# Weight loads on ScalarE's queue and weight preparation in steps, in a two-layer row attention kernel

## The chip, the cores and the metric

The kernel runs on one core of a Trainium2 chip. The metric is the time of one execution on the device in microseconds, as a median over runs; four runs of the kernel before gave 3379.72 us (3377.62 to 3380.11). The profile is one further execution, recorded by the hardware profiler.

The engines are named as in the profile: PE is TensorE (PEld its weight loads), DVE is VectorE, ACT is ScalarE, POOL is GpSimd, SP is SyncE, which only issues transfers. "SPq" and "ACTq" are the queues through which SP and ScalarE issue transfers (DMA). A line number L1144 is line 1144 of the kernel before.

## The reference

The input x has 128 rows of 256 positions with 256 channels, z has 256 x 256 positions with 128 channels. Layer 0 is attention within each row, with a bias worked out from z; layer 1 is banded attention. Cut to what matters here:

```python
def _gn(v, G=32, eps=1e-5):            # mean and variance of a group of 8 channels over all rows and positions
    g = v.reshape(B_, H_, W_, G, C_ // G)
    m = jnp.mean(g, axis=(1, 2, 4), keepdims=True)
    s = jnp.var(g, axis=(1, 2, 4), keepdims=True)
    return ((g - m) / jnp.sqrt(s + eps)).reshape(v.shape)

# layer 0, on m = _gn(x)
m_norm = layer_norm(m, ln_m_w, ln_m_b)
z_norm = layer_norm(z, ln_z_w, ln_z_b)
q, k, v = m_norm @ Wq.T, m_norm @ Wk.T, m_norm @ Wv.T        # 8 heads of 32
b = (z_norm @ Wb.T).transpose(0, 3, 1, 2)[:, None]
gate = sigmoid(m @ Wg.T + bg)
scores = einsum('bsihc,bsjhc->bshij', q, k) * scale + b
o = einsum('bshij,bsjhc->bsihc', softmax(scores), v) * gate
x = x + o @ Wo.T + bo

# layer 1, on _gn of the new x: 4 heads of 64, band of 16
qkv = x2 @ w_in.T + b_in
x = x + banded_attention(qkv) @ w_out.T + b_out
```

The group norm needs a sum over the whole of x before the first row can be projected, and the bias needs all of z. So the kernel begins with a pass over all of x and z.

## The kernel before, in words

The kernel is `fast_kernel`, with a general kernel behind it that runs only if a test of value ranges at the end asks for it. It has three parts: the opening (to about 246 us), layer 0 over 64 pairs of rows (to about 2115 us), layer 1 over 64 pairs.

**The weights** (lines 828 to 939). `load_chunks`, `load_col` and `load_row` load a matrix, a vector as columns (elements of 4 bytes) and a vector copied to all partitions. All of them issue through SP's queue, and so do w_out (8 loads), wb, and bv_c (4 loads). They are 27 loads with 2.3 MB in all; wq, wk, wv, wg, wo and w_out have 256 KB each, w_in 768 KB.

**Their preparation** (lines 996 to 1055). The layer norms' weights and biases are folded into the matrices. The products of the biases with wq, wk, wv and wb (`qb`, `kb`, `vb_r`, `bz_r`: lines 998 to 1017) are matrix products on PE, copied out by DVE. Then wq, wk, wv are scaled by `lnw_c` (1020 to 1022), and the mean of their columns, by a product with the constant matrix `avg` on PE (1028), is subtracted on DVE (1030); wb is treated in the same way (1031, 1039, 1040), and four copies of it are laid into `wbz` (1055). Smaller scalings of w_in, bin_c, bg_c and wo come along (1023, 1032 to 1035). The products use the pool `ps_mm`, which has two buffers in PSUM: a third product waits until DVE has read the first.

**The pass over z and x** (lines 1470 to 1492). The order of each engine's instructions between `with tc.manual_schedule()` and its end is the order in which the code is written; instructions outside of it are placed by the scheduler, also among or ahead of those inside. z comes in 16 jobs of 2 MB, x in 8 blocks of 4 MB:

- `z_front` loads a z tile (`zt`, three buffers, line 1061) and takes its statistics on DVE in 16 instructions (1069), then their scale `zrs` (1077 on DVE, 1078 on POOL). After each quarter of the statistics it calls `mark`, at which steps of other work are taken in by a table, `plan`.
- `z_back` of the job before turns the tile on PE (32 transposes, 1091), copies it with ScalarE (1093), and projects it with `wbz` (1106). When the transposes are done, the tile's buffer is free for the job three further on.
- `x_block` loads a block (`xa`, two buffers, 1142) and takes its statistics in 16 instructions on DVE (1144).

Job 0 is followed by x block 0, jobs 2 to 8 each by one of the blocks 1 to 7; job 1 has none. So the order on DVE is z0, x0, z1, z2, x1, z3, x2, z4, x3 and so on to z8, x7, z9 to z15. SP's queue issues the loads in the same order, and each waits there until its buffer is free: z3 until PE has turned z0, x2 until DVE is through with x0. What stands behind a waiting load in the queue waits too.

After x7, `x_moments` (1151 to 1156) merges the sums of x; the table `plan` then spreads the group norm's constants and the first pair's preparation over jobs 9 to 15. When z is done, layer 0 begins.

Line 1616, `bv_w`, belongs to the preparation of layer 1. It multiplies `ones` by `bv_c` on DVE, outside of the hand-written order.

Of the kernel before, what the change touches and what calls it, by code (L numbers as in the profile page):

```python
# [9 lines left out]
F32 = mybir.dt.float32  # L10
AF = mybir.ActivationFunctionType
ALU = mybir.AluOpType
# [4 lines left out]
P = 128  # L17
# [756 lines left out]
def fast_kernel(  # L774
# [46 lines left out]
    ones = const.tile([P, P], F32, name="ones")  # L821
    nc.vector.memset(ones, 1.0)
    avg = const.tile([P, P], F32, name="avg")
# [3 lines left out]

    def load_chunks(src, n, name):
        t = const.tile([P, src.shape[0] // P, n], F32, name=name)
        nc.sync.dma_start(t, src.rearrange("(k p) n -> p k n", p=P))  # L830
        return t

    def load_col(src, name):
        t = const.tile([P, src.shape[0] // P], F32, name=name)
        nc.sync.dma_start(t, src.rearrange("(k p) -> p k", p=P))
        return t

    def load_row(src, name):
        n = src.shape[0]
        t = const.tile([P, n], F32, name=name)  # L840
        nc.sync.dma_start(t, src.unsqueeze(0).broadcast_to([P, n]))
        return t


# [63 lines left out]

    eb = const.tile([P, H, NB, I], F32, name="eb")

    wq = load_chunks(wqT, C, "wq")
    wk = load_chunks(wkT, C, "wk")
    wv = load_chunks(wvT, C, "wv")
    wg = load_chunks(wgT, C, "wg")
    wo = load_chunks(woT, C, "wo")
    w_in = load_chunks(w_inT, 3 * C, "w_in")

    w_out = const.tile([P, KC, C], F32, name="w_out")
    for a in range(KC):
        for h in range(H1):  # L920
            n = P // H1
            nc.sync.dma_start(w_out[h * n : (h + 1) * n, a, :], w_outT[(2 * h + a) * n : (2 * h + a + 1) * n, :])
    wb = const.tile([CZ, H], F32, name="wb")
    nc.sync.dma_start(wb, wbT)
    lnw_c = load_col(ln_m_w, "lnw_c")
    lnb_c = load_col(ln_m_b, "lnb_c")
    lzw_c = load_col(ln_z_w, "lzw_c")
    lzb_c = load_col(ln_z_b, "lzb_c")
    bg_c = load_col(bg, "bg_c")
    bin_c = load_col(b_in[0 : 2 * C], "bin_c")  # L930
    bo_r = load_row(bo, "bo_r")
    bv_c = const.tile([P, KC], F32, name="bv_c")
    for h in range(H1):
        n = P // H1
        nc.sync.dma_start(
            bv_c[h * n : (h + 1) * n, :],
            b_in[2 * C + h * D1 : 2 * C + (h + 1) * D1].rearrange("(a i) -> i a", i=n),
        )
    bout_r = load_row(b_out, "bout_r")

    qb = const.tile([P, KC], F32, name="qb")
    kb = const.tile([P, KC], F32, name="kb")
    vb_r = const.tile([P, C], F32, name="vb_r")
    bz_r = const.tile([P, H], F32, name="bz_r")
# [12 lines left out]
    def group_pairs(src, g):  # L957

        return src[:, :, g * GE : (g + 2) * GE].rearrange("p n (h e) -> p n e h", h=2)
# [27 lines left out]
    pz = tc.alloc_tile_pool(name="pre_z", bufs=1, side="right")  # L987
# [4 lines left out]
    def mm(name):  # L992
        return ps_mm.tile([P, 512], F32, name=name, tag="mm")


    lnb_w = pz.tile([P, KC, P], F32, name="lnb_w")
    for k in range(KC):
        nc.vector.tensor_scalar_mul(lnb_w[:, k, :], ones, lnb_c[:, k : k + 1])
    for w, dst in ((wq, qb), (wk, kb)):
        for m in range(KC):  # L1000
            ps = mm("b_ps")
            for k in range(KC):
                nc.tensor.matmul(
                    ps[:, 0:1], w[:, k, m * P : (m + 1) * P], lnb_c[:, k : k + 1],
                    start=(k == 0), stop=(k == KC - 1),
                )
            nc.vector.tensor_copy(dst[:, m : m + 1], ps[:, 0:1])
    nc.vector.tensor_scalar_mul(qb, qb, QS)
    ps = mm("b_ps")
    for k in range(KC):  # L1010
        nc.tensor.matmul(ps[:, :C], lnb_w[:, k, :], wv[:, k, :], start=(k == 0), stop=(k == KC - 1))
    nc.vector.tensor_copy(vb_r, ps[:, :C])
    lzb_w = pz.tile([P, P], F32, name="lzb_w")
    nc.vector.tensor_scalar_mul(lzb_w, ones, lzb_c)
    ps = mm("b_ps")
    nc.tensor.matmul(ps[:, :H], lzb_w, wb, start=True, stop=True)
    nc.vector.tensor_copy(bz_r, ps[:, :H])

    for k in range(KC):
        nc.vector.tensor_scalar(wq[:, k, :], wq[:, k, :], lnw_c[:, k : k + 1], QS, ALU.mult, ALU.mult)  # L1020
        nc.vector.tensor_scalar_mul(wk[:, k, :], wk[:, k, :], lnw_c[:, k : k + 1])
        nc.vector.tensor_scalar_mul(wv[:, k, :], wv[:, k, :], lnw_c[:, k : k + 1])
        nc.vector.tensor_scalar_mul(w_in[:, k, 0:C], w_in[:, k, 0:C], QS1)

    for w in (wq, wk, wv):
        ps = mm("b_ps")
        for k in range(KC):
            nc.tensor.matmul(ps[:, :C], avg, w[:, k, :], start=(k == 0), stop=(k == KC - 1))
        for k in range(KC):
            nc.vector.scalar_tensor_tensor(w[:, k, :], ps[:, :C], -1.0 / KC, w[:, k, :], ALU.mult, ALU.add)  # L1030
    nc.vector.tensor_scalar_mul(wb, wb, lzw_c)
    nc.vector.tensor_scalar_mul(bin_c[:, 0:KC], bin_c[:, 0:KC], QS1)

    nc.vector.tensor_scalar_mul(bg_c, bg_c, 0.5)
    nc.vector.tensor_scalar_mul(wo.rearrange("p k n -> p (k n)"), wo.rearrange("p k n -> p (k n)"), 0.5)


    ps = mm("b_ps")
    nc.tensor.matmul(ps[:, :H], avg, wb, start=True, stop=True)
    nc.vector.tensor_sub(wb, wb, ps[:, :H])  # L1040

    nga = S // GA
    st0 = pz.tile([P, nga, G, 3], F32, name="st0")
# [5 lines left out]
    IB, IS = 32, 64  # L1049
    zjobs = [(b, i) for b in range(NB) for i in range(0, I, IB)]  # L1050
    z_rows = z.rearrange("(u t) (p b) c -> t p u (b c)", t=NB, b=NB)
    wbz = pz.tile([P, 4, 4, H], F32, name="wbz")
    nc.vector.memset(wbz, 0.0)
    for j in range(4):
        nc.vector.tensor_copy(wbz[:, j, j, :], wb)

    def z_front(b, i0):

        nonlocal zrs
        zt = pz.tile([P, IB, CZ], F32, name="zt", tag="zt", bufs=3)  # L1060
        nc.sync.dma_start(
            zt.rearrange("p (u b) c -> p u (b c)", b=NB), z_rows[b, :, i0 // NB : (i0 + IB) // NB, :]
        )

        st = pz.tile([P, IB, 3], F32, name="zst", tag="zst", bufs=2)
        for i in range(0, IB, 2):
            if i % (IB // 4) == 0 and i:
                mark(i // (IB // 4))
            nc.vector.bn_stats(
                st[:, i : i + 2, :].rearrange("p i f -> p (i f)"),  # L1070
                zt[:, i : i + 2, :].rearrange("p i c -> p c i"),
            )
        at = i0 % IS
        if at == 0:
            zrs = pz.tile([P, IS], F32, name="zrs", tag="zrs", bufs=3)
        rs = zrs[:, at : at + IB]
        nc.vector.tensor_scalar(rs, st[:, :, 2], 1.0 / CZ, 1e-5, ALU.mult, ALU.add)
        nc.gpsimd.tensor_tensor(rs, rs, mhalf[:, :IB], ALU.pow)
        return zt, zrs
# [60 lines left out]
    def x_block(j):  # L1140
        xa = px.tile([P, GA * NB, C], F32, name="xa", tag="xa", bufs=2)
        nc.sync.dma_start(xa, x[j * GA : (j + 1) * GA].rearrange("s i c -> (s i) c").rearrange("(p n) c -> p n c", p=P))
        for g in range(0, G, 2):
            nc.vector.bn_stats(st0[:, j, g : g + 2, :].rearrange("p g f -> p (g f)"), group_pairs(xa, g))  # L1144

    def x_moments():
# [316 lines left out]
    ended = None  # L1463

    def mark(quarter):
        if ended is not None:
            plan.pop((n - ended, quarter), nothing)()


    behind, nx, n = None, 0, 0  # L1470
    with tc.manual_schedule():
        for n, job in enumerate(zjobs):
            front = z_front(*job)
            if behind is not None:
                z_back(*behind)
            behind = (*job, *front)
            if nx < nga and nx * 9 <= n * nga:
                x_block(nx)
                nx += 1
                if nx == nga:  # L1480
                    ended = n
            mark(4)
        assert not plan
        z_back(*behind)
        z_project()
        z_exp()
# [14 lines left out]
    with tc.manual_schedule():  # L1501
        old = was = Nobody()
        es = nn3 = None
        for p in range(NP):
# [3 lines left out]
            ps = now.scores(0, 0)  # L1508
# [15 lines left out]
            ps = now.scores(0, 1)  # L1524
# [13 lines left out]
            ps = now.scores(1, 0)  # L1538
# [12 lines left out]
            ps = now.scores(1, 1)  # L1551
# [52 lines left out]
    with tc.tile_pool(name="l1", bufs=2) as sb, tc.tile_pool(  # L1604
        name="l1s", bufs=4
# [310 lines left out]
```

## Time and profile before

| | us |
|---|---|
| median of four runs | 3379.72 |
| profiled execution | 3377.75 |
| its span, first to last instruction | 3375.9 |
| first z load issued / landed for DVE | 17.58 / 28.25 |
| preparation of the weights on DVE | 14.44 to 27.24 |
| statistics of x block 0 / block 7 begin | 38.03 / 155.20 |
| first scores of layer 0 used by DVE (line 1305) | 247.00 |

Busy time over the whole span: PE 3229.2 us (96%), DVE 2027.1 (60%), POOL 1973.0 (58%), ACT 1463.1 (43%); the DMA engines moved 262.89 MB. The 40 equal slices of the span (84 us each) show that the beginning differs from the rest: in tenths of busy time PE has 5, 3, 8, 9 and then 9 throughout, DVE 7, 9, 6, 6, and the DMA engines 9, 9, 5, 1 and then 1 or 2.

In a row of the timeline stand the start, the time from the first start to the last end, the engine, the line, the operation, what it writes and reads, how many instructions are merged into the row, and in brackets how long the engine was idle before it and what ended that. The tables of windows give the busy time of each engine in a stretch, the number of instructions in brackets, then the granted TensorE clock, the busy share of the DMA engines and the rate in GB/s. A DMA queue's line has its packets, MB, and the time of its packets as a share of 16 engines.

### The profile page before, as it was taken

What the parts mean: (1) busy time and instruction counts of PE and PEld (TensorE: products, weight loads), DVE (VectorE), ACT (ScalarE), POOL (GpSimd) and SP (SyncE); (2) the same over time, 40 slices, a digit from 0 to 9 for tenths busy, and PEclk for the clock granted to TensorE, in tenths of its full rate; (3) what the DMA queues carried; (4) which work ended last, traced back from release to release, by engine and by line L of the source; (5) the groups of instructions that cost most, each with busy time, mean ns of one, the idle gap of its engine ahead of it and who ended that gap; (6) DMA issues with size and microseconds to landing.
All of it is one profiled execution on the core that took longest, in us unless ns stands there. A gap on an engine that the chain in (4) does not pass through costs nothing. (4 is left out here: it accounts for less than half of the span.)

```text
span 3375.9 us, 81186 instructions
## 1 busy us (share of the span) xinstructions
PE 3229.2 (96%) x35158; PEld 2036.5 (60%) x35158; DVE 2027.1 (60%) x3218; ACT 1463.1 (43%) x2121; POOL 1973.0 (58%) x1377
## 2 busy tenths in 40 slices
PE   5389999999999999999999998899999999999998
PEld 3255555555555555555555554576767767777676
DVE  7966666666666666666666666366544344444456
ACT  2264444444444444444444443344444444444443
POOL 2378877777777877877777784333333333333332
PEclk8799999999999999999999999899999999999999
DMA  9951212221221222222222211121121211211211
GB/s 333 382 135 42 73 48 74 73 73 49 73 70 47 67 70 73 48 73 73 73 48 73 73 55 57 56 65 53 54 63 52 64 54 52 65 52 58 59 58 53
DMA packets 198815, 262.89 MB, mean 78 GB/s; under 512 B 46289, under 2 KB 147537, under 8 KB 197297
## 3 DMA queue, kind: packets, MB, share of 16 engines
q1 hardware_dynamic: 197776, 257.35, 25.1%
q8 instruction: 278, 4.55, 0.7%
q14 instruction: 89, 0.72, 0.1%
q10 hardware_dynamic: 672, 0.26, 0.0%
HBM read 188.82 MB, written 68.75 MB: 76 GB/s over the span
## 5 line engine op out<-in xcount | busy, mean ns | idle before, releaser
L1310 POOL TENSOR_TENSOR eboth<-e 128x512 f32<-128x512 f32 x512 | 639.8, 1271 | 377.7 <-DVE e L1305 365.8
L1305 DVE TENSOR_TENSOR e<-ps_sc,eb 128x1024 f32<-128x1024 f32 x512 | 603.2, 1220 | 316.0 <-ACT ps_sc L1296 226.8
L1296 ACT ACTIVATE ps_sc<-ps_sc 128x1024 f32<-128x1024 f32 x512 | 492.8, 1006 | 507.5 <-PE ps_sc L1289 507.5
L1705 POOL TENSOR_TENSOR e<-e,bw 128x384 f32<-128x384 f32 x256 | 259.0, 1033 | 443.3 <-ACT e L1703 443.3
L1666 PE MATMUL ps_p<-xgT,w_in 128*128 128x512 f32 x1024 | 469.4, 601 | 0.0
L1658 POOL TENSOR_TENSOR xt<-xt,bout_r 128x1024 f32<-128x1024 f32 x64 | 152.3, 2379 | 383.9 <-PE ps_x L1655 383.9
L1758 DVE TENSOR_TENSOR yo<-ps_y,xt 128x512 f32<-128x512 f32 x128 | 88.4, 690 | 379.2 <-PE ps_y L1754 370.8
L1666 PEld LDWEIGHTS ps_p<-xgT,w_in 128*128 128x128 f32 x1024 | 188.9, 190 | 199.9 <-issue 166.6
L1289 PE MATMUL ps_sc<-qT,kT 32*128 32x256 f32 x4096 | 293.8, 400 | 2.0 <-ACT kT L1259 2.0
L1320 PE MATMUL ps_ov<-e,v 128*32 128x256 f32 x4096 | 274.1, 385 | 0.5 <-DVE oT L1334 0.5
L1255 PE MATMUL ps_p<-xnT,wq 128*128 128x512 f32 x512 | 254.3, 618 | 0.8 <-POOL xnT L1242 0.6
L1255 PE MATMUL ps_p<-xgT,wg 128*128 128x512 f32 x512 | 253.9, 618 | 0.0
L1754 PE MATMUL ps_y<-w_out,oT 128*128 128x256 f32 x1024 | 248.6, 386 | 2.6 <-DVE oT L1739 2.6
L1362 PE MATMUL ps_y<-wo,oT 128*128 128x256 f32 x1024 | 243.6, 381 | 7.0 <-POOL oT L1352 7.0
L1362 PEld LDWEIGHTS ps_y<-wo,oT 128*128 128x128 f32 x1024 | 195.4, 191 | 87.9 <-issue 59.5
L1289 PEld LDWEIGHTS ps_sc<-qT,kT 32*128 32x128 f32 x4096 | 185.4, 184 | 94.4 <-issue 70.8
L1270 PE MATMUL ps_v<-wv,xnT 128*128 128x256 f32 x1024 | 242.1, 379 | 0.0
L1255 PE MATMUL ps_p<-xnT,wk 128*128 128x512 f32 x512 | 240.6, 592 | 0.0
L1681 PE MATMUL ps_v<-w_in,xgT 128*128 128x256 f32 x1024 | 231.8, 379 | 0.0
L1736 DVE RECIPROCAL rv<-odd 128x256 f32<-128x256 f32 x128 | 224.4, 1753 | 4.4
L1681 PEld LDWEIGHTS ps_v<-w_in,xgT 128*128 128x128 f32 x1024 | 194.4, 190 | 53.5 <-issue 30.1
L1270 PEld LDWEIGHTS ps_v<-wv,xnT 128*128 128x128 f32 x1024 | 189.6, 190 | 50.9 <-issue 31.1
(163 smaller groups left out, 4992.0 us busy)
## 6 DMA issues: line engine op xcount, KB each, us to landing
zt<-in_z_dram SPq DMA_DIRECT2D x16, 2048.0 KB
xa<-in_x_dram SPq DMA_DIRECT2D x8, 4096.0 KB
xt<-in_x_dram SPq DMA_DIRECT2D x64, 512.0 KB
rvb<-rsum SPq DMA_DIRECT2D x256, 128.0 KB
x<-xo SPq DMA_DIRECT2D x16, 2048.0 KB
xt<-x SPq DMA_DIRECT2D x64, 512.0 KB
out_dram<-yo SPq DMA_DIRECT2D x63, 512.0 KB
rs_r<-rs_d SPq DMA_DIRECT2D x63, 256.0 KB
```

The lines of the kernel that those rows point to most:

```text
L1255: nc.tensor.matmul(ps, w[:, k, m * P : (m + 1) * P], getattr(self, src)[:, k, :], start=(k == 0), stop=(k == KC - 1),)
L1270: nc.tensor.matmul(self.ps_v[:, b * C : (b + 1) * C], self.xnT[:, k, t * P : (t + 1) * P], wv[:, k, :], start=(k == 0), stop=(k == KC - 1),)
L1289: nc.tensor.matmul(self.pss[q // 2][:, q % 2, b, :], self.kT[rs, c, r * I + b * P : r * I + (b + 1) * P], self.qT[rs, c, r * I : (r + 1) * I],
L1296: nc.scalar.activation(self.pss[a], self.pss[a], AF.Exp)
L1305: nc.vector.tensor_tensor(e, pss[a], eb[:, h : h + 2], ALU.mult)
L1310: nc.gpsimd.tensor_tensor(t, es[a][:, :, 0, :], es[a][:, :, 1, :], ALU.add)
L1320: nc.tensor.matmul(ov[q * D0 : (q + 1) * D0, :], self.v[:, r, b, h * D0 : (h + 1) * D0], es[q // 2][:, q % 2, b, :], start=(b == 0), stop= ...
L1362: nc.tensor.matmul(self.ps_y[:, b * C : (b + 1) * C], self.oT[r][:, k, b * P : (b + 1) * P], wo[:, k, :], start=(k == 0), stop=(k == KC - 1),)
L1666: nc.tensor.matmul(ps, w_in[:, k, n * C + m * P : n * C + (m + 1) * P], self.xgT[:, k, :], start=(k == 0), stop=(k == KC - 1),)
L1681: nc.tensor.matmul(ps[:, b * C : (b + 1) * C], self.xgT[:, k, t * P : (t + 1) * P], w_in[:, k, 2 * C : 3 * C], start=(k == 0), stop=(k == ...
L1705: nc.gpsimd.tensor_tensor(e[:, q], e[:, q], bcast(bw.rearrange("p b w -> p (b w)"), 1, KC), ALU.mult)
L1754: nc.tensor.matmul(ps[:, b * C : (b + 1) * C], self.oT[r][:, k, b * P : (b + 1) * P], w_out[:, k, :], start=(k == 0), stop=(k == KC - 1),)
```

## The change

Three things are changed.

1. All weight loads are issued through ScalarE's queue (`nc.scalar.dma_start`) instead of SP's, and their order is new: lnb_c, wq, wk, wv, wb, lnw_c, lzw_c, lzb_c, wg, wo, w_in, w_out, bg_c, bin_c, bo_r, bv_c, bout_r. So SP's first loads are z tile 0 and x block 0.
2. Tile 0 of z is loaded as two halves, each with a transfer of its own.
3. The preparation becomes a generator, `weights()`, whose steps are taken inside of the hand-written order: three among the statistics of x block 0 (after each quarter but the last), three at the quarters of z job 1, and one at the end of job 1. Between two steps PE makes the products that the next one reads. `z_back` of job 0, the first user of `wbz`, comes after step 6.

```diff
     def load_chunks(src, n, name):
-        nc.sync.dma_start(t, src.rearrange("(k p) n -> p k n", p=P))
+        nc.scalar.dma_start(t, src.rearrange("(k p) n -> p k n", p=P))
...
+    def weights():
+        lnb_w = pz.tile([P, KC, P], F32, name="lnb_w")
         for k in range(KC):
+            nc.vector.tensor_scalar_mul(lnb_w[:, k, :], ones, lnb_c[:, k : k + 1])
+        for w, dst in ((wq, qb), (wk, kb)):
+            pss = []
+            for m in range(KC):
+                ps = mm("b_ps")
+                for k in range(KC):
+                    nc.tensor.matmul(
+                        ps[:, 0:1], w[:, k, m * P : (m + 1) * P], lnb_c[:, k : k + 1],
+                        start=(k == 0), stop=(k == KC - 1),
+                    )
+                pss.append(ps)
+            yield
+            for m in range(KC):
+                nc.vector.tensor_copy(dst[:, m : m + 1], pss[m][:, 0:1])
+        nc.vector.tensor_scalar_mul(qb, qb, QS)
+        ps_v = mm("b_ps")
...
+        ps_z = mm("b_ps")
+        nc.tensor.matmul(ps_z[:, :H], lzb_w, wb, start=True, stop=True)
+        yield
+        nc.vector.tensor_copy(vb_r, ps_v[:, :C])
+        nc.vector.tensor_copy(bz_r, ps_z[:, :H])
+        for k in range(KC):
+            nc.vector.tensor_scalar(wq[:, k, :], wq[:, k, :], lnw_c[:, k : k + 1], QS, ALU.mult, ALU.mult)
+            nc.vector.tensor_scalar_mul(wk[:, k, :], wk[:, k, :], lnw_c[:, k : k + 1])
+            nc.vector.tensor_scalar_mul(wv[:, k, :], wv[:, k, :], lnw_c[:, k : k + 1])
+        nc.vector.tensor_scalar_mul(wb, wb, lzw_c)
+        for ws in ((wq, wk), (wv,)):
+            pss = []
+            for w in ws:
+                ps = mm("b_ps")
+                for k in range(KC):
+                    nc.tensor.matmul(ps[:, :C], avg, w[:, k, :], start=(k == 0), stop=(k == KC - 1))
+                pss.append(ps)
+            if ws == (wv,):
+                ps_b = mm("b_ps")
+                nc.tensor.matmul(ps_b[:, :H], avg, wb, start=True, stop=True)
+            yield
+            for w, ps in zip(ws, pss):
+                for k in range(KC):
+                    nc.vector.scalar_tensor_tensor(w[:, k, :], ps[:, :C], -1.0 / KC, w[:, k, :], ALU.mult, ALU.add)
+        nc.vector.tensor_sub(wb, wb, ps_b[:, :H])
+        nc.vector.memset(wbz, 0.0)
+        for j in range(4):
+            nc.vector.tensor_copy(wbz[:, j, j, :], wb)
+        yield
...
+    def z_front(b, i0, first):
...
+        n = 2 if first else 1
+        for u in range(n):
+            part = slice(u * IB // n, (u + 1) * IB // n)
+            nc.sync.dma_start(
+                zt[:, part].rearrange("p (u b) c -> p u (b c)", b=NB),
+                z_rows[b, :, (i0 + part.start) // NB : (i0 + part.stop) // NB, :],
+            )
...
         for g in range(0, G, 2):
+            if g % (G // 4) == 0 and g:
+                next(prepare, None)
             nc.vector.bn_stats(st0[:, j, g : g + 2, :].rearrange("p g f -> p (g f)"), group_pairs(xa, g))
...
     def mark(quarter):
+        if n > 0:
+            next(prepare, None)
...
+    prepare = weights()
     with tc.manual_schedule():
         for n, job in enumerate(zjobs):
-            front = z_front(*job)
+            front = z_front(*job, n == 0)
```

After the last `yield`, step 7 holds the scalings of w_in, bin_c, bg_c and wo, as before. The arithmetic of every operand is unchanged.

More of the change, by code (lines that the diff above doesn't have):

```diff
@@ L834, in load_col @@
         t = const.tile([P, src.shape[0] // P], F32, name=name)
-        nc.sync.dma_start(t, src.rearrange("(k p) -> p k", p=P))
+        nc.scalar.dma_start(t, src.rearrange("(k p) -> p k", p=P))
         return t
@@ L840, in load_row @@
         t = const.tile([P, n], F32, name=name)
-        nc.sync.dma_start(t, src.unsqueeze(0).broadcast_to([P, n]))
+        nc.scalar.dma_start(t, src.unsqueeze(0).broadcast_to([P, n]))
         return t
@@ L909, in fast_kernel @@
     eb = const.tile([P, H, NB, I], F32, name="eb")
+    lnb_c = load_col(ln_m_b, "lnb_c")
     wq = load_chunks(wqT, C, "wq")
@@ L913, in fast_kernel @@
     wv = load_chunks(wvT, C, "wv")
+    wb = const.tile([CZ, H], F32, name="wb")
+    nc.scalar.dma_start(wb, wbT)
+    lnw_c = load_col(ln_m_w, "lnw_c")
+    lzw_c = load_col(ln_z_w, "lzw_c")
+    lzb_c = load_col(ln_z_b, "lzb_c")
     wg = load_chunks(wgT, C, "wg")
@@ L921, in fast_kernel @@
             n = P // H1
[L922 to L928, printed above, removed]
+            nc.scalar.dma_start(w_out[h * n : (h + 1) * n, a, :], w_outT[(2 * h + a) * n : (2 * h + a + 1) * n, :])
     bg_c = load_col(bg, "bg_c")
@@ L934, in fast_kernel @@
         n = P // H1
-        nc.sync.dma_start(
+        nc.scalar.dma_start(
             bv_c[h * n : (h + 1) * n, :],
@@ L993, in mm @@
         return ps_mm.tile([P, 512], F32, name=name, tag="mm")
[L996 to L1023, printed above, removed]
@@ L1025, in fast_kernel @@
-    for w in (wq, wk, wv):
-        ps = mm("b_ps")
-        for k in range(KC):
-            nc.tensor.matmul(ps[:, :C], avg, w[:, k, :], start=(k == 0), stop=(k == KC - 1))
-        for k in range(KC):
[L1030 to L1035, printed above, removed]
@@ L1038, in fast_kernel @@
-    ps = mm("b_ps")
-    nc.tensor.matmul(ps[:, :H], avg, wb, start=True, stop=True)
-    nc.vector.tensor_sub(wb, wb, ps[:, :H])
+    def weights():
+        lnb_w = pz.tile([P, KC, P], F32, name="lnb_w")
+        for k in range(KC):
+            nc.vector.tensor_scalar_mul(lnb_w[:, k, :], ones, lnb_c[:, k : k + 1])
[14 more added lines that the diff above has]
+        ps_v = mm("b_ps")
+        for k in range(KC):
+            nc.tensor.matmul(ps_v[:, :C], lnb_w[:, k, :], wv[:, k, :], start=(k == 0), stop=(k == KC - 1))
+        lzb_w = pz.tile([P, P], F32, name="lzb_w")
+        nc.vector.tensor_scalar_mul(lzb_w, ones, lzb_c)
+        ps_z = mm("b_ps")
[27 more added lines that the diff above has]
+        yield
+        for k in range(KC):
+            nc.vector.tensor_scalar_mul(w_in[:, k, 0:C], w_in[:, k, 0:C], QS1)
+        nc.vector.tensor_scalar_mul(bin_c[:, 0:KC], bin_c[:, 0:KC], QS1)
+        nc.vector.tensor_scalar_mul(bg_c, bg_c, 0.5)
+        nc.vector.tensor_scalar_mul(wo.rearrange("p k n -> p (k n)"), wo.rearrange("p k n -> p (k n)"), 0.5)
@@ L1052, in fast_kernel @@
     wbz = pz.tile([P, 4, 4, H], F32, name="wbz")
[L1053 to L1057, printed above, removed]
+    def z_front(b, i0, first):
         nonlocal zrs
         zt = pz.tile([P, IB, CZ], F32, name="zt", tag="zt", bufs=3)
-        nc.sync.dma_start(
-            zt.rearrange("p (u b) c -> p u (b c)", b=NB), z_rows[b, :, i0 // NB : (i0 + IB) // NB, :]
-        )
+        n = 2 if first else 1
[5 more added lines that the diff above has]
+            )
         st = pz.tile([P, IB, 3], F32, name="zst", tag="zst", bufs=2)
```

## The prediction

> **What bounds the kernel now.** I first read the table of stages (window, its length, then PE, PEld, DVE, ACT, POOL busy; granted clock, DMA share, GB/s), because shares of the whole span hide a stage with another limit.
>
> ```profile
> 0.00:17.00 17.00, 2.54 (x12) 2.54 (x13) 2.75 (x17) 1.28 (x1) 2.90 (x15) 1.00 0.52 146
> 60.00:90.00 30.00, 17.12 (x100) 11.08 (x100) 29.97 (x68) 11.68 (x25) 9.68 (x2) 0.77 1.04 402
> ...
> 330.00:360.00 30.00, 30.00 (x238) 17.18 (x231) 18.03 (x27) 13.97 (x18) 23.58 (x17) 1.00 0.18 45
> ```
>
> From about 246 us on PE has no idle time and no line of the change runs there, so the change acts only on when that part begins. In the opening, 30 to 165 us, DVE (29.97 of 30 us) and the DMA engines (share 1.04) are full together; in the first 17 us no engine is. Next the timeline of the SP queue, which shows when loads are issued:
>
> ```profile
> 0.80 0.44 SPq L830 DMA_DIRECT2D wq<-in_wqT_dram  x1
> ...
> 17.58 0.43 SPq L1061 DMA_DIRECT2D zt<-in_z_dram  x1
> 18.06 4.32 SPq L1142 DMA_DIRECT2D xa<-in_x_dram  x1
> 22.42 15.50 SPq L1061 DMA_DIRECT2D zt<-in_z_dram  x2
> 37.97 5.92 SPq L1142 DMA_DIRECT2D xa<-in_x_dram  x1
> 44.06 0.37 SPq L1061 DMA_DIRECT2D zt<-in_z_dram  x1
> ```
>
> 27 weight loads occupy SP's queue for 16.8 us before the first z tile. Then the timeline of DVE, whose statistics are the chain of the opening:
>
> ```profile
> 28.25 5.42 DVE L1069 BATCH_NORM_STATS2 zst<-zt 128x6 f32<-128x256 f32 x16 [1.01 <-DMA zt<-in_z_dram]
> 33.71 0.18 DVE L1077 TENSOR_SCALAR zrs<-zst 128x32 f32<-128x32 f32 x1
> 38.03 9.64 DVE L1144 BATCH_NORM_STATS2 st<-xa 128x6 f32<-128x512 f32 x16 [4.14 <-DMA xa<-in_x_dram]
> ...
> 59.75 9.64 DVE L1144 BATCH_NORM_STATS2 st<-xa 128x6 f32<-128x512 f32 x16 [1.01 <-DMA xa<-in_x_dram]
> ...
> 75.62 9.67 DVE L1144 BATCH_NORM_STATS2 st<-xa 128x6 f32<-128x512 f32 x16
> ...
> 155.20 9.61 DVE L1144 BATCH_NORM_STATS2 st<-xa 128x6 f32<-128x512 f32 x16 [0.48 <-DMA xa<-in_x_dram]
> ```
>
> Between 38.03 and 164.8 us DVE waits only 3.3 us (1.01, 1.32, 0.53, 0.48, all for x blocks). So an earlier start of the loads pays only as far as DVE's own work permits, and that work grows: what DVE did before 27.2 us, in time when it had no tile, now stands inside the full stretch. Last, DMA packets by queue, in 204 to 206 us (q1 is SP's queue, q10 ScalarE's) and in 28 to 34 us:
>
> ```profile
> q1 hardware_dynamic: 633, 0.65, 106.6%
> q10 hardware_dynamic: 501, 0.00, 14.2%
> ```
> ```profile
> DMA packets 79, 2.56 MB, mean 427 GB/s; under 512 B 0, under 2 KB 0, under 8 KB 0
> ```
>
> ScalarE's queue got nearly a packet for each of SP's; a packet of an x block is 32 KB (2.56 MB / 79), one of a z tile 1 KB.
>
> **The change, part by part.** Call T the time at which x block 0 has landed (38.03 us now).
>
> *Loads.* The first z tile (now two halves, one more issue of 0.4 us that the 4.3 us of x's issue hide) is issued at 0.8 instead of 17.58 us. From its issue to x0's landing the trace has 38.03 - 17.58 = 20.45 us, so T = 0.8 + 20.45 = 21.25 us if the weights cost nothing. They do cost: no row has both queues moving megabytes, so I bound it. Above: all weights go first, at the engine time that they take now, the DMA shares of 2 to 10 us (0.90, 0.91, 1.02, 0.82, times 2 us each, 7.3 us) and of 10 to 18 us (0.12, 0.19, 0.27, 0.29, 1.7 us), 9.0 us: T = 30.3. Below: nothing, or even a gain of 1.5 us, because z's first 2 us (18 to 20 us) ran at 99 GB/s behind the last row loads, against 380 later: T = 19.8. I take the value by the packet row, the only one with both queues busy: beside z0's 2048 packets about as many of ScalarE's go, which covers the column loads and wq to wo, 1.3 MB at 348 GB/s (40 to 44 us, 1 KB packets) = 3.8 us; beside x0's 128 packets go 128 of w_in, 0.39 MB at 427 GB/s = 0.9 us. T = 21.25 + 4.7 = 26.0 us.
>
> The row comes first: SP spent 16.8 us on issuing, and the DMA engines were busy for 0.52 of these. Against it stands a rule of the Trainium skill ("DMA: Bandwidth & Descriptors", section "Issuing engines are not separate DMA queues"): loads started by several engines end up on the same 16 DMA engines and interleave, and only the issuing sequencer's time is saved. By the rule the 9.0 us of engine time above stay to be paid, T = 30.3 and a gain of 0.1 us by the sum below; taken as a free second queue, T = 21.25 and 9.2 us. The trace has no row that decides between them at this size.
>
> *ScalarE.* Its queue now carries the 27 issues (16.8 us). They are free because its first copy (29.02 us now) comes after z0's transposes, which move to about T + 20 = 46 us; without that cover each issue would delay a z copy by 0.5 us. POOL issues no load in either version.
>
> *Preparation on DVE.* Steps 1 to 3 stand among x0's statistics, 4 to 6 among z1's, 7 behind them. From the rows of 14 to 27 us: lnb_w 0.48, four copies 0.63, qb 0.16, lzb_w 0.28 (1.55); vb_r 0.42, bz_r 0.16, six scalings 1.65 (five at the 0.26 between starts, one of 0.35), wb 0.23 (2.46); six subtractions of a mean 2.28, wb 0.15, wbz 0.17 + 0.39 (2.99); w_in 0.49, bin and bg 0.34, wo 0.43 (1.26). Sum 8.3 us on the full engine.
>
> *New waits.* PE's products run between steps, under a quarter of statistics: 2.4 us of x (9.64 / 4) covers each of steps 2 and 3 (1.86 to 2.5 us), but 1.36 us of z (5.42 / 4) does not cover wq and wk times avg (24.24 - 20.46 = 3.8 us). wq is there after 2 us, wk 1.9 us later, by which time DVE has done wq's part: 1.0 us of stall. From x0's start to z2's end DVE has 20.7 us now (38.03 to 58.75), so then 20.7 + 8.3 + 1.0 = 30.0, and x2 begins 15.9 later (59.75 to 75.62): **T + 45.9**.
>
> Queued behind these products in PE's hand-written order are z0's transposes, and for them waits the load of z3, which takes z0's buffer; SP's next issue, x2, stands behind z3. x0 with its three steps ends at T + 11.1; a quarter, step 4, a quarter, step 5 end at T + 18.6; wv and wb times avg at T + 20.2; 32 transposes take 5.35 us (28.36 us): z3 is issued at T + 25.6 (51.6 instead of 44.06). The queue is empty by then (z0 to z2, x0, x1 and the weights are 17 MB, at the 385 GB/s of 38 to 60 us through at 47 us), so z3 and x2 need what z0 and x0 needed, 20.45 us: x2 lands at **T + 46.05**, together with DVE. With T = 26.0, x2 starts at 72.0 instead of 75.62: **3.6 us gained**, of the 16.8 us by which the first load moves.
>
> *After x2.* x2 to x7 takes 79.58 us now. DVE alone would need 2.33 us less (three waits), the DMA at 399 GB/s (92 to 155 us) five times 6.29 MB, 78.8 us, 0.8 us less. As the queue has no reserve after z3's late issue I take the DMA's: **0.8 us**, ends 0 and 2.3.
>
> *To the end.* From x7 on (moments, the remaining z tiles, first projections) order and waits stay: PE stands at 167.9 us for x's sums, and the later z buffers come free through it, so everything behind shifts whole. Sum: 3.6 + 0.8 = 4.4 us. The profiled execution took 3377.75 us (span 3375.9 and 1.85 around it) and becomes 3373.35; it lies 1.97 us under the median of the runs, 3379.72, so the forecast for a median is **3375.3 us**.
>
> **Rivals.** Each follows from T: gain = 75.62 - (T + 46.0) + 0.8.
>
> 1. *The weights slip into gaps* (z's slow 2 us, packets of 32 KB that leave little to the other queue). T = 22: 8.4 us, **3371.3**. For it: a DMA share of 0.43 at 18 to 20 us. Against: 1.04 in all full windows.
> 2. *The loads gain nothing*: the weights go first, T = 30.3, gain 0.1, **3379.6**. For it: their 9.0 us of engine time. Against: the packet row.
> 3. *Slower: a late small weight holds DVE.* Line 1616 (bv_w, needs bv_c) is outside the hand-written order and stands at 23.25 us among the preparation now, so its place is the scheduler's. bv_c is next to last on ScalarE's queue. If bv_w stands ahead of z0's statistics, DVE waits for bv_c: its packets come after x0's 32 KB ones, about 4 us after x0's landing, 30 us; z0 5.6, so x0 starts at 35.6 and the sum is 75.62 - 81.6 + 0.8 = -5.2: **3384.9**. It costs from the point at which bv_c lands after 24.8 us (30.4 - 5.6). Against: it stands behind its load now and waits for nothing.
>
> **How the numbers follow.** Forecast 0.52, rival 1 0.25, rival 2 0.10, rival 3 0.13. 0.2% (6.8 us) is about what a measurement of this kernel can tell from no change: faster needs under 3373.0. Rival 1 gives 0.22 of its 0.25 and the early end of the forecast (T under 23.7) 0.10: 0.32. Slower over 3386.5 needs bv_c after 31.6 us: 0.07. The rest, 0.61, lies within. The range reaches from a little under rival 1 to past rival 2, with a part of rival 3 left out: 3370.0 to 3381.8. The forecast's own range is 3372.5 to 3379.
>
> **What would show it.** In the changed profile: zt's first issue at 0.8 us; x0's statistics starting near 26 us; steps 4 to 6 among z1's with about 1 us of waits for PE; z3's issue near 52 us, later than 44.06; x2's statistics near 72; x7's near 150 (155.20). x0 at 22 means rival 1, at 30 rival 2; a wait of DVE for bv_c, or any weight, rival 3. The prediction is wrong in kind if DVE shows waits for z3 or x2 of more than 3 us, or if the stretch from x7 to the first scores does not keep its length.

## The result, and the profile after

The changed kernel is slower: 3382.21 us (median; 3380.49 to 3384.65) against 3379.19 us for the kernel before on the same chips, a ratio of 1.001 with a 95% interval of 1.0005 to 1.0015. Its profiled execution has a span of 3381.4 us, before 3375.9. A loss of 0.1% is half of what I took to be the least that can be told, but over this many runs the interval leaves no change out. The forecast was 3375.3 us, faster; the sign is wrong and the time lies just outside the range.

First the table of stages of the changed kernel (window, its length, then PE, PEld, DVE, ACT, POOL busy; granted clock, DMA share, GB/s):

```profile
0.00:17.00 17.00, 1.83 (x8) 1.78 (x8) 6.29 (x25) 0.00 (x0) 3.48 (x16) 1.00 0.88 272
17.00:28.00 11.00, 0.00 (x0) 0.00 (x0) 0.00 (x0) 0.00 (x0) 4.89 (x1) 1.00 0.88 363
28.00:36.00 8.00, 0.00 (x0) 0.00 (x0) 0.00 (x0) 1.28 (x1) 0.00 (x0) 1.00 0.72 134
36.00:60.00 24.00, 13.16 (x60) 10.90 (x60) 21.43 (x66) 3.10 (x7) 0.16 (x1) 1.00 0.86 318
...
330.00:360.00 30.00, 30.00 (x228) 17.24 (x227) 18.29 (x30) 13.61 (x17) 24.01 (x18) 1.00 0.16 46
```

The early start of the loads is there: 272 GB/s in the first 17 us instead of 146. But from 17 to 36 us DVE does not work at all (0.00 of 19 us), and from 28 to 36 us the DMA engines, 0.72 of the time occupied, move only 134 GB/s. The last row is unchanged in kind: PE is full, so once more only the opening differs.

Then the timeline of the SP queue after, as shown of before:

```profile
0.80 1.07 SPq L1077 DMA_DIRECT2D zt<-in_z_dram  x2
12.60 0.34 SPq L1159 DMA_DIRECT2D xa<-in_x_dram  x1
30.23 4.62 SPq L1077 DMA_DIRECT2D zt<-in_z_dram  x2
34.89 6.51 SPq L1159 DMA_DIRECT2D xa<-in_x_dram  x1
60.19 0.37 SPq L1077 DMA_DIRECT2D zt<-in_z_dram  x1
```

z0 goes out at 0.80 instead of 17.58 us, but x0 only at 12.60, and z1 at 30.23, 7.8 us *later* than before (22.42). And the timeline of DVE after:

```profile
7.78 2.74 DVE L1086 BATCH_NORM_STATS2 zst<-zt 128x6 f32<-128x256 f32 x8 [6.18 <-DMA zt<-in_z_dram]
13.34 2.74 DVE L1086 BATCH_NORM_STATS2 zst<-zt 128x6 f32<-128x256 f32 x8 [2.82 <-DMA zt<-in_z_dram]
16.11 0.18 DVE L1094 TENSOR_SCALAR zrs<-zst 128x32 f32<-128x32 f32 x1
38.05 0.48 DVE L1638 TENSOR_SCALAR bv_w<-ones,bv_c 128x128 f32<-128x128 f32 x2 [21.76 <-DMA bv_c<-in_b_in_dram]
38.45 2.47 DVE L1163 BATCH_NORM_STATS2 st<-xa 128x6 f32<-128x512 f32 x4
...
66.19 9.72 DVE L1163 BATCH_NORM_STATS2 st<-xa 128x6 f32<-128x512 f32 x16
...
82.14 9.66 DVE L1163 BATCH_NORM_STATS2 st<-xa 128x6 f32<-128x512 f32 x16
...
159.09 9.60 DVE L1163 BATCH_NORM_STATS2 st<-xa 128x6 f32<-128x512 f32 x16
```

The fourth row shows what holds x0. Line 1638 (1616 before), the preparation of `bv_w` for layer 1, stands between z0 and x0, and DVE waits 21.76 us for `bv_c`. x0's statistics have no bracket: their block had landed before (near 26 us, as an experiment below shows). They begin at 38.45, where the kernel before began at 38.03.

So the ledger of the opening is this. x0 begins 0.42 us later than before. From x0 to x1 the time is 27.74 us instead of 21.72: seven us of preparation are now in that stretch, and the wait of 1.01 us ahead of x1 is gone. x2 begins 6.5 us later (82.14 against 75.62). From x2 to x7 DVE no longer waits for any x block and wins back 2.6 us (76.95 against 79.58), so x7 is 3.9 us late. The stretch to the first scores is 1.5 us longer (252.39 - 159.09 = 93.30, before 91.80), which makes 5.4 of the 5.5 us between the spans. The spans are of one execution each; the medians are 3.0 us apart, and single executions of one kernel spread by about 4 us, so the ledger is good for the order of the opening and not for its last two or three us. What DVE did before 27 us at no cost, because it had no tile, it now does in the full stretch, and the time in which it used to do it stands empty.

### The profile page after: what moved, and what is told of

Read it like the earlier page. It is cut to its first block, busy times and chain, and to the rows that moved or that the text cites. A ratio compares the mean times of both kernels' runs of the same rounds, so it can differ in the third digit from the quotient of the medians.

```text
span 3381.4 us, 81186 instructions
## 1 busy us (share of the span) xinstructions
PE 3225.8 (95%) x35158; PEld 2032.0 (60%) x35158; DVE 2024.9 (60%) x3218; ACT 1465.1 (43%) x2121; POOL 1974.3 (58%) x1377
```

## The experiments

**My theory** after this result: (a) `bv_w`'s wait eats what the early loads bring; (b) behind it the loads have an order of their own, in which small weights hold back z1. **The rival**: the preparation that was moved into the full stretch costs the time, whichever way the loads go. The kernels of the experiments are called e1 to e7 and e9. Each is the changed kernel with the edit shown, and its ratio is to the kernel before, measured beside it.

### Take the wait for bv_c away

In e1 `bv_w` gets a place of its own, in step 7 of the preparation.

```diff
+    bv_w = const.tile([P, KC, P], F32, name="bv_w")
     def weights():
...
         nc.vector.tensor_scalar_mul(wo.rearrange("p k n -> p (k n)"), wo.rearrange("p k n -> p (k n)"), 0.5)
+        for k in range(KC):
+            nc.vector.tensor_scalar_mul(bv_w[:, k, :], ones, bv_c[:, k : k + 1])
...
-        bv_w = const.tile([P, KC, P], F32, name="bv_w")
-        for k in range(KC):
-            nc.vector.tensor_scalar_mul(bv_w[:, k, :], ones, bv_c[:, k : k + 1])
```

> Edit: bv_w (two products of ones with bv_c on DVE) is moved out of the scheduler's hands into step 7 of the preparation, behind z job 1. Theory (a late small weight holds DVE): x0 had landed near 27.5 us and only bv_w, waiting for bv_c until 38.05, held it. Then x0's statistics start at 27.5 to 28.5 us instead of 38.45; z1, issued at 30.2, becomes the next wait (2 to 4 us), x1 starts near 58 (66.19), x7 near 151 (159.09), and the time falls by 7 to 9 us, to about 3374, ratio to before 0.998 to 0.999. Rival A (the loads share the DMA engines with the weights and x0 itself landed at 36 to 38): x0's statistics start at 36 or later, now with a wait for x, and the time stays at 3381 to 3383. Rival B (the 7 us of preparation on the full DVE are the loss): x0 starts earlier but x1 and x7 move by less than 3 us.

Ratio to the kernel before 0.9994 (0.9985 to 1.0003). DVE's timeline of this kernel:

```profile
25.88 2.48 DVE L1167 BATCH_NORM_STATS2 st<-xa 128x6 f32<-128x512 f32 x4 [9.46 <-DMA xa<-in_x_dram]
...
39.83 1.42 DVE L1090 BATCH_NORM_STATS2 zst<-zt 128x6 f32<-128x256 f32 x4 [3.41 <-DMA zt<-in_z_dram]
...
57.53 9.76 DVE L1167 BATCH_NORM_STATS2 st<-xa 128x6 f32<-128x512 f32 x16
...
73.50 9.66 DVE L1167 BATCH_NORM_STATS2 st<-xa 128x6 f32<-128x512 f32 x16
...
152.98 9.61 DVE L1167 BATCH_NORM_STATS2 st<-xa 128x6 f32<-128x512 f32 x16 [1.36 <-DMA xa<-in_x_dram]
```

The one line moved, x0's statistics begin 12.6 us earlier. So `bv_w` was what held them, and (a) is shown. But of these 12.6 us only 8.7 are left at x1 (57.53 against 66.19), 8.6 at x2 and 6.1 at x7 (152.98 against 159.09). A first part goes into a new wait: 3.41 us for z1, which is still issued at 30.03 us. The time missed what was expected: the ratio is 0.0016 under the changed kernel's, 5.4 us and not 7 to 9.

The same thing from the other side, e2: the load of `bv_c` goes first on ScalarE's queue.

```diff
+    bv_c = const.tile([P, KC], F32, name="bv_c")
+    for h in range(H1):
+        n = P // H1
+        nc.scalar.dma_start(
+            bv_c[h * n : (h + 1) * n, :],
...
     lnb_c = load_col(ln_m_b, "lnb_c")
```

> Edit: the four loads of bv_c are the first on ScalarE's queue; bv_w stays where the scheduler puts it, which is now ahead of z0's statistics. Theory (a late small weight holds DVE): bv_c is there by about 4 us, so bv_w holds nothing, and the time is that of the kernel with bv_w in step 7 to within 2 us (four more issues of 0.45 us stand ahead of wq): x0 near 28 to 29.5 us, time 3374 to 3376. Rival A (loads are slow): x0 at 36 or later, 3381 to 3383. If it were bv_w's place and not its load that costs, this kernel would stay at 3382 and only the other would gain.

Ratio 0.9990 (0.9980 to 0.9999). The scheduler now puts `bv_w` ahead of z0 (it runs at 9.53 us after a wait of 7.93), x0 begins at 23.38, 2.5 us before e1's, and yet x1 at 57.25, 0.3 before e1's: z1 is issued at 28.73, and the wait for it is 6.04 us. What x0 gains, z1 takes away. `bv_c` lands later than expected (9.53 us, not 4) and x0 earlier (28 to 29.5). The line is still outside of the hand-written order and the loss is gone, so it was its late load that cost.

### One half of the change at a time

e3 keeps the steps and puts the loads back on SP's queue; e4 keeps the loads on ScalarE's queue and takes all steps ahead of the hand-written order. z0's two halves are in both and were not tested alone.

```diff
-        nc.scalar.dma_start(t, src.rearrange("(k p) n -> p k n", p=P))
+        nc.sync.dma_start(t, src.rearrange("(k p) n -> p k n", p=P))
...
```

> Edit: all weight loads go back to SP's queue, ahead of z and x; the preparation stays spread in steps. Theory: DVE gets x0 near 38 to 39 us as in the changed kernel, so this one is the changed kernel without the early loads, and as these are wasted there, the time is the same to within 1.5 us, 3380.5 to 3384; x1 near 66, z3's issue near 60. Rival A (the sharing of the DMA engines between two queues costs): this kernel is faster than the changed one by 2 us or more, since no queue is shared.

Ratio 1.0006 (0.9997 to 1.0015). With all loads back on SP, ahead of z, and the preparation still in steps, x0 begins at 36.41 us (38 to 39 expected), x2 at 80.11 (75.62 before) and x7 at 157.10 (155.20). DVE now idles 16.10 us for `bv_c` and 5.47 us for z0 at the start, without the preparation that filled this time. From x0 to x7 it takes 120.7 us, before 117.2: the steps by themselves make the pass over x 3.5 us longer. The time as a whole can't be told from no change, nor from the changed kernel's.

```diff
     prepare = weights()
+    for _ in prepare:
+        pass
     with tc.manual_schedule():
```

> Edit: the loads stay on ScalarE's queue and z and x first, but all steps of the preparation are emitted ahead of the hand-written order, as in the kernel before; the scheduler puts them among z0's statistics, and bv_w again ahead of x0's. Theory: bv_w holds x0 until 37 to 39 us as in the changed kernel, but the preparation is done by then, so x1 starts near 59 to 60 (66.19), nothing waits for x after it, and the time is 3376 to 3379, 4 to 6 us under the changed kernel and 0 to 3 under the one before. Rival B (preparation on the full DVE is the loss) expects the same here; rival A expects x0 at 36 to 38 with a wait for x instead of bv_c.

Ratio 0.9993 (0.9984 to 1.0002). The other half alone: loads as in the changed kernel, all preparation ahead of the hand-written order. DVE's timeline:

```profile
36.91 0.48 DVE L1640 TENSOR_SCALAR bv_w<-ones,bv_c 128x128 f32<-128x128 f32 x2 [4.47 <-DMA bv_c<-in_b_in_dram]
37.31 9.71 DVE L1163 BATCH_NORM_STATS2 st<-xa 128x6 f32<-128x512 f32 x16
...
57.99 9.65 DVE L1163 BATCH_NORM_STATS2 st<-xa 128x6 f32<-128x512 f32 x16
...
73.85 9.67 DVE L1163 BATCH_NORM_STATS2 st<-xa 128x6 f32<-128x512 f32 x16
...
152.03 9.61 DVE L1163 BATCH_NORM_STATS2 st<-xa 128x6 f32<-128x512 f32 x16 [0.80 <-DMA xa<-in_x_dram]
```

Although `bv_w` still waits for `bv_c` and x0 begins only at 37.31, x1 and x2 come within 0.5 us of e1's and x7 1.0 us earlier. The time before x0 is enough for the whole preparation.

So the loss has two parts, and taking out either one undoes it: without the wait (e1) or without the steps (e4) the kernel is no longer slower. The rival holds in part: the wait makes x0 late, and the preparation behind it keeps DVE from making that good.

By the order of the opening, what the change wins, it wins by the queue; the steps add work to the full stretch and win nothing. In time neither half alone is clear of no change.

### Why z1 comes late

The waits of SP's queue in the changed kernel's first 70 us (engine, line, waited for: us in total, times, longest):

```profile
SPq L1077 <- PE ps_t L1108: 22.1, 2, 18.7
SPq L1077 <- DMA bg_c<-in_bg_dram: 17.3, 1, 17.3
SPq L1159 <- DMA wv<-in_wvT_dram: 10.7, 1, 10.7
...
SPq L1077 <- DMA bin_c<-in_b_in_dram: 0.2, 1, 0.2
```

Neither load needs these weights, and yet x0 waits for wv and z1 for bg_c. The waits fit one rule: with the loads of both queues counted in one common order, an issue waits until the load eight places earlier has landed. Behind bg_c come bin_c, bo_r, four loads of bv_c and bout_r, so z1 is the eighth; z2 is then the eighth behind bin_c, and for that one SP's queue waits too. Where the rule comes from the traces don't show. Before, the same kind of wait cost 3.7 us inside of the weights (w_out for w_in 2.5, wo 0.9, wg 0.3) and never stood ahead of z or x. Now ScalarE's queue is in the chain as well: by the same count its seventh w_out load waits for x0 and its eighth for w_in. They go out at 25.97 and 27.75 us (in e1 the seventh goes out at 25.88, the moment at which x0's statistics begin; in e2, too, a w_out load goes out at that moment, 23.38), and bg_c, bin_c, bo_r and the four loads of bv_c only after them. bg_c is issued at 28.10 us, and z1 goes at 30.23. The small loads themselves are slow. The changed kernel's packets by queue from 28 to 32 us (q10 is ScalarE's queue; packets, MB, share of 16 engines):

```profile
DMA packets 921, 0.10 MB, mean 25 GB/s; under 512 B 827, under 2 KB 921, under 8 KB 921
...
q10 hardware_dynamic: 917, 0.10, 47.6%
```

917 packets, most of them under 512 bytes (columns of 4-byte elements), take 47.6% of the engines for 0.10 MB. With the engines nearly empty from 28 to 30 us (a share of 0.17), this is where the 134 GB/s of the stage table come from. It also fits that bv_c, issued from 29.66 us on, reaches DVE only at 38.05.

If that is right, layer 1's loads need only leave the opening. e5 issues w_in, w_out, bin_c, bv_c and bout_r (15 of the 27 loads) in layer 0's loop and scales them there, long before layer 1 uses them:

```diff
-    w_in = load_chunks(w_inT, 3 * C, "w_in")
...
+    def load_layer1():
+        nc.sync.dma_start(w_in, w_inT.rearrange("(k p) n -> p k n", p=P))
...
+            if p == 8:
+                load_layer1()
+            if p == 12:
+                scale_layer1()
             nxt.root()
```

> Edit: the weights that only layer 1 needs (w_in, w_out in 8 loads, bin_c, bv_c in 4 loads, bout_r: 15 loads) are loaded through SP in layer 0's loop and scaled there, with bv_w; ScalarE's queue keeps 12 loads. Theory (a load is issued only when the one eight places before it in the common order of both queues has landed, so many small loads keep z1 and x1 back): z1 is issued near 13 us instead of 30, right behind x0, and has landed when x0's statistics end, so the wait of 3.4 us for z1 that the kernel with bv_w in step 7 showed is gone; x0 starts at 25 to 26.5, x1 at 52 to 54 (57.5 there), x2 at 67.5 to 70 (73.5), x7 at 146 to 149 (153), ratio to before 0.9970 to 0.9985. Rival (z1 waits for the DMA engines, which are full, and not for its issue): z1's wait stays at 2 to 4 us, x1 at 56 to 58, ratio as there, 0.9990 to 0.9997.

Ratio 0.9975 (0.9965 to 0.9985): clearly faster than before. SP's queue and DVE:

```profile
13.74 12.20 SPq L1084 DMA_DIRECT2D zt<-in_z_dram  x2
```
```profile
35.91 1.41 DVE L1093 BATCH_NORM_STATS2 zst<-zt 128x6 f32<-128x256 f32 x4
...
52.66 9.75 DVE L1170 BATCH_NORM_STATS2 st<-xa 128x6 f32<-128x512 f32 x16
...
148.62 9.61 DVE L1170 BATCH_NORM_STATS2 st<-xa 128x6 f32<-128x512 f32 x16 [1.63 <-DMA xa<-in_x_dram]
```

x0 begins at 25.46 us, as in e1, but z1 is issued at 13.74 and its statistics follow x0's without a wait. x1 begins at 52.66, x2 at 68.65, x7 at 148.62, each within what was expected, and the rival falls. Of the 4.4 us by which x0 to x1 is shorter than in e1, 3.4 are the wait for z1 and 1.0 the scalings of w_in, bin_c and `bv_w`, which left the opening with the loads.

The same wait can be set up at will. In e9 the 15 loads go out on SP's own queue, right behind x1:

```diff
-            if p == 8:
-                load_layer1()
...
+                if nx == 2:
+                    load_layer1()
```

> The kernel of e5_layer1_later, but layer 1's 15 loads are issued on SP's queue right behind x block 1, in the opening, and not in layer 0's loop. Nothing is left out. My theory: a load is issued only when the load eight places earlier has landed, in one queue as over two. The seventh w_out load then waits for x block 1, which lands near 48 us, and the last of the fifteen wait for each other, so that z3, which PE would allow at 46.9 us as in e5, is issued at 50 to 57 us, x2's statistics start at 70 to 74, x7's at 150 to 154, ratio to the kernel before 0.998 to 0.9995. Rival: there is no such rule, the fifteen cost only their issue (15 times 0.4 to 0.6 us, over before 46.9) and 1 MB in the queue (2.6 us): z3 at 46.9 to 47.5 us, x2 at 69 to 71, x7 at 149 to 151.3, ratio 0.997 to 0.9985.

Ratio 0.9999 (0.9989 to 1.0008). Up to x1 this kernel agrees with e5 to 0.1 us (52.70). The timeline of its SP queue, and what that queue waited for:

```profile
33.78 18.32 SPq L936 DMA_DIRECT2D w_out<-in_w_outT_dram  x8
...
55.13 0.39 SPq L1084 DMA_DIRECT2D zt<-in_z_dram  x1
```
```profile
SPq L936 <- DMA xa<-in_x_dram: 9.4, 1, 9.4
SPq L936 <- DMA zt<-in_z_dram: 3.2, 1, 3.2
SPq L936 <- DMA w_in<-in_w_inT_dram: 2.3, 1, 2.3
```

Eight loads of 32 KB take 18.32 us to issue, because one waits 9.4 us for an x block and others for z and w_in. z3 goes out at 55.13 us (46.85 in e5), inside the 50 to 57 expected, and the rival's 46.9 to 47.5 falls. The price was underrated: x2 begins at 76.35 (70 to 74 expected) and x7 at 155.14 (150 to 154), 6.5 us behind e5, and the ratio lies above the 0.998 to 0.9995 expected. In the trace the DMA engines are idle but for a share of 0.17 from 52 to 56 us.

### Put the preparation into DVE's empty time

Steps 1 to 6 are taken among and right behind z0's statistics, while DVE waits for x0; in e6 with layer 1's loads in the loop, in e7 with all loads as in the changed kernel (and `bv_w` in step 7).

```diff
     def mark(quarter):
-        if n > 0:
+        if quarter < 4 or n > 0:
             next(prepare, None)
...
             front = z_front(*job, n == 0)
+            if n == 0:
+                for _ in range(3):
+                    next(prepare, None)
...
-            if g % (G // 4) == 0 and g:
-                next(prepare, None)
```

> Edit: as the kernel with layer 1's weights later, and steps 1 to 6 are taken among and right behind z0's statistics, while DVE waits for x0. Theory (the preparation is paid in full only because it stands on the full stretch): x0 starts at 26 to 28, x1 near 47 to 49, z0's transposes begin near 26, so z3 is issued near 31 and the queue does not run empty; x2 near 63 to 65, x7 at 141 to 144, ratio to before 0.9955 to 0.9970. Rival (from x1 on the DMA rate of 399 GB/s alone decides, so nothing is won beyond the earlier loads): x2 not before 67, x7 at 146 or later, as in the kernel without this step.

Ratio 0.9968 (0.9955 to 0.9980), 3368.06 us: the lowest time of all, clear of both kernels; its interval overlaps e5's. DVE's timeline of it:

```profile
25.93 9.65 DVE L1168 BATCH_NORM_STATS2 st<-xa 128x6 f32<-128x512 f32 x16 [1.32 <-DMA xa<-in_x_dram]
...
49.76 9.64 DVE L1168 BATCH_NORM_STATS2 st<-xa 128x6 f32<-128x512 f32 x16 [2.67 <-DMA xa<-in_x_dram]
...
66.09 9.70 DVE L1168 BATCH_NORM_STATS2 st<-xa 128x6 f32<-128x512 f32 x16 [0.39 <-DMA xa<-in_x_dram]
...
144.94 9.62 DVE L1168 BATCH_NORM_STATS2 st<-xa 128x6 f32<-128x512 f32 x16 [0.61 <-DMA xa<-in_x_dram]
```

The wait ahead of x0 is down to 1.32 us, and now each of these blocks waits for its load. From x1 to x7 these waits come to only 1.9 us, so DVE and the loads are nearly level, with the loads a little behind. That they are behind at all is why it missed in part. z3 was expected near 31 us and issued at 33.32; x1 and x2 were expected at 47 to 49 and 63 to 65 us and came 0.8 and 1.1 us late, x7 0.9 us past its 141 to 144. The ratio is inside what was expected, and the rival (x2 not before 67, x7 at 146 or later) falls: x7 comes 3.7 us before e5's.

> Edit: bv_w in step 7, and steps 1 to 6 among and behind z0's statistics; all loads as in the changed kernel. Theory: x0 at 26 to 28, then a wait for z1 (issued at 30, landed near 39.8) of 2 to 4 us, z1 and z2 without steps, and a wait for x1, which is issued at 33 to 40 and needs some 17 us: x1 at 53 to 57, x2 at 69 to 73, x7 at 149 to 152, ratio 0.9980 to 0.9990, between the kernel with bv_w in step 7 alone and the one with both.

Ratio 0.9996 (0.9987 to 1.0005), a miss on every point behind x0. x0 begins at 26.80, but z1 is issued at 30.89 and DVE waits 5.72 us for it and 4.01 us for x1 (58.62). Removing seven us of work from DVE's stretch brings nothing here (x7 at 153.79, e1 152.98). I had charged the waits behind z1 too little: with DVE out of the way the queue is what the opening follows. Beside e6, which differs in where layer 1's weights are loaded and scaled (`bv_w` with them), x7 is 8.9 us later.

The changed kernel once more, in one set with e5, e6 and e7:

> The changed kernel itself, beside the next three on the same chip. Expected as before: ratio to the kernel before 1.0005 to 1.0015, x7 at 158 to 160 us.

Ratio 1.0010 (1.0001 to 1.0019). `bv_w` runs at 38.31 us after a wait of 21.73, x7 begins at 159.40 and the first scores are used at 252.47: the order of the opening repeats to 0.3 us.

## Why the prediction was wrong, step by step

| step of the forecast | predicted | changed kernel | e1 (bv_w moved) |
|---|---|---|---|
| x0's statistics begin (T) | 26.0 | 38.45 | 25.88 |
| x0 to x1 | 30.0 | 27.74 | 31.65 |
| z3's issue after x0's start | 25.6 | 21.74 | 24.90 |
| x2 begins | 72.0 | 82.14 | 73.50 |
| x2 to x7 | 78.8 | 76.95 | 79.48 |
| x7 to the first scores | 91.80 | 93.30 | 89.80 |

**The step that failed is the choice between the forecast and rival 3.** The prediction named the line, its missing place in the hand-written order, its late load, and "a wait of DVE for bv_c" as the sign; then it gave the case 0.13, with the argument that the line "stands behind its load now and waits for nothing". So in the forecast itself the wait was put at nothing, on the strength of the line's place in the kernel before, which came from a scheduler that saw another program. In the four kernels here that leave it to the scheduler it was put ahead of z0 (e2, e3) or between z0 and x0 (the changed kernel, e4), and waited in all of them. In the changed kernel DVE waited 21.76 us for bv_c and x0 began at 38.45 instead of 26.0; with the line moved (e1) it began at 25.88. With that wait gone the rest of the forecast isn't refuted by the time: it had a gain of 4.4 us, a ratio of 0.9987, and e1's 0.9994 has an interval of 0.9985 to 1.0003.

**The price of rival 3** was wrong in two ways that cancel in part. I put `bv_w` ahead of z0, with z0's 5.6 us still to do behind it; it stood behind z0. I had bv_c landing at 30 us, four after x0; it came at 38.05, because it was issued only from 29.66 us on. The rival's own row gave 3384.9 us, a loss of 5.2 where 3.0 was measured; its x0 at 35.6 stands against 38.45. That the time isn't further out is luck: x0 came 2.9 us later than in the rival, but the preparation behind it was cheaper than in the sum, and x2 to x7 shorter.

**The loads: T was right, its packet count too, but in part by luck.** With the wait for bv_c gone x0 begins at 25.88, against 26.0 from the packet row; the free queue (21.25) and the weights first (30.3) are both out by over four us. The packets went as the row said: from 2 to 12 us of the changed kernel SP's queue has 2061 and ScalarE's 1856, from 18 to 20 us, beside x0, 28 and 27. But the sum let x0's issue follow z0's, and it waited for wv until 12.60 us. No run isolates what that wait cost x0, so the agreement to 0.1 us is in part luck. The rule of the Trainium skill ("DMA: Bandwidth & Descriptors", section "Issuing engines are not separate DMA queues"), by which only issue time is saved, is neither borne out nor refuted at this size: x0 comes 25.88 - 21.25 = 4.6 us after the free queue's time, and how much of this is weight transfers (9.0 us in all) and how much the wait for wv stays open. The same page (section "Queues, rings and completion order") states that each DMA engine takes turns between the queues packet by packet. The trace agrees: from 18 to 20 us of e6, x0's queue and ScalarE's have 30 packets each, 0.98 MB in the one and under 0.01 in the other; in the next two stretches of 2 us they have 26 and 26, 24 and 24.

```profile
q1 hardware_dynamic: 30, 0.98, 113.7%
q10 hardware_dynamic: 30, 0.00, 0.8%
```

This is what I read out of 204 to 206 us, but I used it only for x0. For the small load behind it, the same row means that it crawls at one packet for each 32 KB of x: 30 packets in 2 us here, against 917 in the 4 us in which ScalarE's queue had the engines nearly alone.

**What the loads' step left out** is the order of the issues behind z0. I counted issue times and buffers, and took z1's issue to follow x0's. In truth x0 had to wait for wv (12.60 us) and z1 for bg_c (30.23). e1 shows the price: a wait of 3.41 us for z1. That wait is in no line of the forecast. e1's x7 (152.98) is 2.2 us behind the 150.8 forecast (155.20 - 4.4); 1.65 of them arise between x0 and x1, where this wait is partly made up for by a cheaper preparation, and most of the rest between x2 and x7.

**Preparation on DVE** was sized too high: 8.3 us of work and 1.0 of stall. The changed kernel has 27.74 - 20.71 = 7.0 us, of it 0.44 us of waiting for PE. Most of my rows were durations; the steps from start to start are shorter (`vb_r` to the end of step 3's scalings: 50.21 to 52.30, 2.09 us where the sum had 2.46). z3's issue came early for the same reason and because the 32 transposes took 3.93 us, not 5.35. Where this work goes was the larger mistake. It was costed at a full engine's price, correctly, but I did not ask what the forecast itself implied: that DVE would be empty from the end of z0 until 26 us, long enough for all of it. e6 does that.

**x2 to x7** was taken as 78.8, limited by transfers. In the changed kernel it is 76.95, DVE's own time without waits, because everything starts so late that the transfers are ahead; in e1, where they limit, it is 79.48, so the expected 0.8 us from a full queue did not come.

**To the end.** From the first scores on nothing changed: 3128.9 us to the end of the span before, 3129.0 after. The stretch from x7 to the first scores did not keep its length; it was 89.2 to 94.0 us over all these kernels, for the changed one 93.30 and, repeated, 93.07. What sets it within these 5 us wasn't tried and stays open; as single executions of one kernel spread by about 4 us, a part of it may belong to the execution and not to the kernel.

## What to carry to other kernels

An instruction that stands outside of a hand-written order can be put ahead of anything; if its load becomes late, give it a place, or it may hold its engine (here DVE for 21.76 us, 12.6 of them after x0 had landed, for 0.48 us of work that is needed some 2000 us later). When loads are moved between queues, list which earlier load each issue waits for, and keep loads that are not needed soon out of the common order: leaving 15 of them for later was worth more than the whole rest of the change (e5's ratio 0.9975, e1's 0.9994). Before work is spread over a full stretch, look for the stretch that the change has just emptied, and for what will hold the engine once that work is gone: in e7 the late loads took all of it back, in e6 they no longer could.

## What was unexpected of the hardware and the program

- In this program a load's issue waits for the load eight places earlier even if that one is on the other queue: 17.3 us for z1, 10.7 us for x0, 9.4 us for a w_out load of 32 KB in e9.
- Loads of 4-byte elements cost the DMA engines far more than their bytes: 0.10 MB in 917 packets, most of them under 512 bytes, took 47.6% of all 16 engines for 4 us (25 GB/s), while a stream mostly of 1 KB packets ran at 345 GB/s a few us later (36 to 40 us).
- Two queues share an engine by packets and not by bytes: 30 packets each, with 32 KB in one queue's and a few bytes in the other's.
